# The diagonals of B for TensorE's products: fetched whole from DRAM instead of being built by ScalarE (four-layer visual state-space model, one core)

## The chip, the cores and the metric

The kernel runs on one core of a Trainium2 chip. The metric is the device time of one execution in microseconds, the median of several runs. In the profile PE is TensorE, DVE VectorE, ACT ScalarE, POOL GpSimd, and SP is SyncE, whose queue issues all of this kernel's DMAs.

## The reference

The input is 4 images of 64 x 64 positions with 128 channels. Layers 0, 1 and 3 are selective-scan layers, layer 2 is a gated layer made of matrix products. What matters here is the scan inside a selective-scan layer, cut to its core:

```python
xs = jnp.stack([x0, x1, x0[..., ::-1], x1[..., ::-1]], axis=1)   # 4 directions, 256 channels, 4096 steps
x_dbl = jnp.einsum('bkdl,kcd->bkcl', xs, x_proj_w)
dts, Bs, Cs = jnp.split(x_dbl, [R, R + N], axis=2)               # R = 8, N = 16 states
delta = jax.nn.softplus(jnp.einsum('bkrl,kdr->bkdl', dts, dt_w) + dt_b[None, :, :, None])
def step(h, t):
    x_t, d_t, B_t, C_t = t
    h = jnp.exp(d_t[..., None] * A) * h + (d_t * x_t)[..., None] * B_t[:, :, None, :]
    return (h, jnp.einsum('bkdn,bkn->bkd', h, C_t))
```

For each of the 16 states n and each channel the scan needs, at every step, a decay exp(delta A), an addend delta x B_n, and afterwards a product with C_n summed over the states. B_n and C_n depend on the step and not on the channel. All arithmetic is in float32.

## The kernel before, in words

**Chunks and periods.** The images are taken in two pairs, the three scan layers in turn, which makes 12 turns of one image and one layer. A turn has 4 directions of 8 chunks, and a chunk is 512 steps of 256 channels (two halves m of 128 partitions): 384 chunks. A chunk is worked through in 8 periods, 3,072 in all. Period i takes 4 of the 16 states (quarter q = i // 2) for one of the two halves. Directions 2 and 3 run backward over the same positions ("back" chunks) and use rows that a forward chunk left in DRAM.

**A period.** ACT makes four decays `da` (`decay`, L854). DVE makes four scans `h` (`scan`, L870), two on "side 0" and two on "side 1". For side 0 the addend comes from TensorE: `pair_db` (L845) multiplies the transposed `duT` (delta x) with diagonal matrices of B, so that one product gives delta x B_n for two states at once, in the PSUM tile `dbp`, of which there is one. For side 1 ACT copies delta x into PSUM (`lift`, L862) and DVE multiplies it there with B's rows `bb`, spread over all partitions (L983, L984). POOL multiplies `h` with C's rows `cb` (`times_c`, L882) into `hc`; in periods 0, 2, 4 and 6 it also adds the two sides (L884). PE sums `hc` over the states in `yp` (`add_up`, L895), always that of the period before. ACT saves the last column of `h` as `state` (L878).

**The diagonals.** `diagonals` (L837) builds one block `diag` for a quarter: 4 groups of 128 steps, in each the 128 x 128 identity scaled by B's column of two states, interleaved. ACT does this in 8 scalings of [128 x 128], two of every four in a period; each takes its scale from `bt`, the transpose of B's rows, which PE makes with four transposes (L797) in the prologue and ACT copies out of PSUM (L802). The blocks have two buffers.

**The rest of the work.** While a chunk runs, `prologue` prepares the next one piece by piece (at the half periods listed in `PIECES`): it loads `xs`, projects it to `xd` (8 rows of dt, 16 of B, 16 of C, for two directions) or loads `xd` from DRAM for a back chunk, makes `delta` (softplus with two table loads on ACT), stores `xd` to DRAM (`xd_d`), and makes `du` (POOL) and `duT` (PE, ACT). `spread` (L821) fetches `bb` (512 KB) and `cb` (1 MB) for a quarter from `xd_d`, one row for all partitions; each has two buffers. Between these the steps of the other layers' work run (`between`, called through `other`): norms, products, convolution, and their loads and stores, among them `x_col_d` (L430), stored in pieces of 32 bytes.

**What sets the order.** The program is scheduled by hand: every engine, and SP's queue, executes its instructions in the order in which this code writes them, and waits in place for what it needs. SP therefore waits, in its one queue, for buffers to come free.

Of the kernel before, what the change touches and what calls it, by code (L numbers as in the profile page):

```python
# [13 lines left out]
F32 = mybir.dt.float32  # L14
AF = mybir.ActivationFunctionType
# [14 lines left out]
WP = W + 2  # L30

CQ = 4

PAIRED = (0, 2, 4, 6)

# [29 lines left out]
def vss_stack_kernel(ctx: ExitStack, tc: tile.TileContext, x: bass.AP, weights, out: bass.AP, n_batch=B, layers=(0, 1, 2, 3)):  # L65
# [640 lines left out]
        return [S[a:z] for a, z in zip([0] + marks[1:], marks[1:] + [len(S)])]  # L706


    turns = []
    for e in range(0, n_batch, 2):  # L710
        for i in (0, 1, 3):
# [2 lines left out]
    for turn, (e, i) in enumerate(turns):  # L714

        for nth, k in enumerate((1, 3, 0, 2) if turn else (0, 1, 3, 2)):
            for ci in range(NCH):
                s = SimpleNamespace(turn=turn, e=e, v=wt[i], layer=i, nth=nth, k=k, ci=ci)
                s.c = NCH - 1 - ci if k >= 2 else ci
                s.columns, s.back = k % 2 == 1, k >= 2  # L720
                s.end = 0 if s.back else CH - 1
                s.step = slice(None, None, -1 if s.back else 1)
                s.first, s.last = ci == 0, ci == NCH - 1
                s.flip = len(chunks) % 2
                s.diag, s.cb, s.bb, s.h, s.hc = {}, {}, {}, {}, {}
                chunks.append(s)
    per_turn = K * NCH

# [27 lines left out]
    def scans(pool, ring, deep, psum):  # L756
# [4 lines left out]
        def prologue(s):  # L761


            lane, v = lanes[s.e % 2], s.v
            s.xs = ring.tile([P, 2, CH], F32, tag="xs", name="xs")
            nc.sync.dma_start(out=s.xs, in_=(lane.x_col if s.columns else lane.x_row)[:, :, cols(s.c)])
            if s.first:
                s.dt = pool.tile([R, DI], F32, tag="dt", name="dt_w")
                nc.sync.dma_start(out=s.dt, in_=weights[s.layer][1][:, s.k * DI : (s.k + 1) * DI])
            yield  # L770


            s.xd_d = lane.xd[s.k % 2][s.c]
            s.xd = pool.tile([2 * NX, CH], F32, tag="xd", name="xd")
            if s.back:
                nc.sync.dma_start(out=s.xd[:NX], in_=s.xd_d[1])
                yield
            else:
                ps = psum.tile([P, CH], F32, tag="misc", name="ps_x")
                for m in range(2):  # L780
                    nc.tensor.matmul(ps[: 2 * NX], v["xp"][:, s.k % 2, m, :], s.xs[:, m], start=(m == 0), stop=(m == 1))
                yield
                nc.scalar.copy(s.xd, ps[: 2 * NX])
            s.delta = pool.tile([P, 2, CH], F32, tag="delta", name="delta")
            halves = (s.flip, 1 - s.flip)
            for m in halves:
                ps = psum.tile([P, CH], F32, tag="misc", name="ps_dt")
                nc.tensor.matmul(ps, s.dt[:, m * P : (m + 1) * P], s.xd[:R], start=True, stop=True)  # L788
                yield
                func = AF.Identity if m == halves[0] else AF.Softplus  # L790
                nc.scalar.activation(s.delta[:, m], ps, func, bias=v["dtb"][:, s.k, m : m + 1])  # L791
            m = halves[0]
            nc.scalar.activation(s.delta[:, m], s.delta[:, m], AF.Softplus)  # L793
            nc.scalar.preload_act_table_set("natural_log_exp_and_others")
            ps = psum.tile([P, 4, NX], F32, tag="misc", name="ps_bt")
            for j in range(4):
                nc.tensor.transpose(ps[:, j, :], s.xd[:NX, j * P : (j + 1) * P], ident[:NX, :NX])  # L797
            yield
            if not s.back:
                nc.sync.dma_start(out=s.xd_d.rearrange("k r t -> (k r) t"), in_=s.xd)  # L800
            s.bt = pool.tile([P, 4, N], F32, tag="bt", name="bt")
            nc.scalar.copy(s.bt, ps[:, :, R : R + N])  # L802
            s.du = pool.tile([P, 2, CH], F32, tag="du", name="du")
            for m in halves:
                nc.gpsimd.tensor_mul(s.du[:, m], s.delta[:, m], s.xs[:, m])  # L805
                yield
            s.duT = pool.tile([P, 4, 2, P], F32, tag="duT", name="duT")
            for m in halves:
                ps = psum.tile([P, 4, P], F32, tag="misc", name="ps_duT")
                for j in range(4):  # L810
                    nc.tensor.transpose(ps[:, j, :], s.du[:, m, j * P : (j + 1) * P], ident)  # L811
                yield
                nc.scalar.copy(s.duT[:, :, m, :], ps)  # L813
            yield
# [13 lines left out]
            q = i // 2  # L828
            return q, (i + q + s.flip) % 2

        def diagonals(s, q, half):

            if half == 0:
                s.diag[q] = pool.tile([P, 4, P, 2], F32, tag="diag", name="diag")
            for t in (2 * half, 2 * half + 1):
                for j in range(2):
                    nc.scalar.activation(  # L837
                        s.diag[q][:, t, :, j], ident, AF.Copy, scale=s.bt[:, t, CQ * q + j : CQ * q + j + 1]
                    )

        def pair_db(s, i):
            q, m = place(s, i)
            s.db = psum.tile([P, CH, 2], F32, tag="dbp", name="dbp")
            for t in range(4):
                nc.tensor.matmul(  # L845
                    s.db[:, t * P : (t + 1) * P, :], s.duT[:, t, m, :], s.diag[q][:, t], start=True, stop=True
                )
# [74 lines left out]
        pro = prologue(s)  # L922
        for _ in pro:
            pass
        for q, half in ((0, 0), (0, 1), (1, 0)):
            diagonals(s, q, half)
        spread(s, 0, 0)
        spread(s, 0, 1)
        pair_db(s, 0)
# [5 lines left out]
        for at, (s, i) in enumerate(periods):  # L935
            then = periods[at + 1] if at + 1 < len(periods) else None
            if i == 0:
                nxt = chunks[at // 8 + 1] if at // 8 + 1 < len(chunks) else None
                if nxt:
                    pro, nxt.dt = prologue(nxt), s.dt  # L940
                s.state = pool.tile([P, 2, N], F32, tag="state", name="state") if s.first else before[0].state
                if at % (8 * per_turn) == 0:
                    segments = [(steps, len(steps), frm, to) for steps, frm, to in meanwhile(s.turn)]

            def piece(number):

                if nxt and number in PIECES:
                    next(pro)

            def other(number):  # L950

                gone = at % (8 * per_turn) * 4 + number
                for todo, count, frm, to in segments:
                    while todo and count - len(todo) < count * (gone - frm) / (to - frm):
                        todo.pop(0)()

            da_next = [None, None]
            spreads = (s, i // 2 + 1) if i < 7 else (nxt, 0)
            if i % 2 == 0 or not spreads[0]:
                spreads = None  # L960
            if then:
                da_next[0] = decay(*then, 0)
            if before:
                save(*before, 1)
            if spreads:
                spread(*spreads, 0)
            scan(s, i, 0, 0, da[0], s.db[:, :, 0])
            other(0)
            scan(s, i, 0, 1, da[0], s.db[:, :, 1])
            times_c(s, i, 0)  # L970
            if before:
                add_up(*before, 0)
            if then:
                pair_db(*then)
            piece(2 * i)
            other(1)
            if spreads:
                spread(*spreads, 1)
            if then:
                da_next[1] = decay(*then, 1)  # L980
            save(s, i, 0)
            du, db = dv[i % 2], dv[1 - i % 2]
            nc.vector.tensor_mul(db, du, s.bb[i // 2][:, 0])  # L983
            nc.vector.tensor_mul(du, du, s.bb[i // 2][:, 1])  # L984
            scan(s, i, 1, 0, da[1], db)
            other(2)
            scan(s, i, 1, 1, da[1], du)
            times_c(s, i, 1)
            if then:
                lift(*then)  # L990

            q, half = (i + 2 + i % 2) // 2, 1 - i % 2
            if q < 4:
                diagonals(s, q, half)
            elif nxt:
                diagonals(nxt, q - 4, half)
            if i < 2 and full:
                leave(*full.pop(0))
            if before:
                add_up(*before, 1)  # L1000
            piece(2 * i + 1)
            other(3)
            da = da_next
            before = (s, i)
            if then and then[0].turn != s.turn:
                assert not any(todo for todo, *_ in segments)
# [101 lines left out]
```

## Time and profile before

| | |
|---|---|
| median of 3 runs | 22,745.52 us (22,731.7 to 22,749.28) |
| the profiled execution | 22,741.48 us; its span 22,739.6 us |
| TensorE's granted clock, mean | 0.959 |
| busy | PE 87%, DVE 86%, POOL 85%, ACT 82% |
| DMA | 3,060 MB in 2,437,559 packets, 42.5% of the 16 engines' time |
| ACT, scalings for diag (L837) | 12,288 of 401 ns, 3,952.1 us |
| POOL, hc (L882) | 6,144 of 2,361 ns, 14,411.8 us |
| DVE, scans (L870) | 12,288 of 1,201 to 1,263 ns |
| bb and cb loads (L821) | 1,536 of 512 KB and 1,536 of 1,024 KB |

A row of a group gives its line, engine, operation, output <- inputs, shapes and count, then busy time and the mean of one, then how long the engine stood idle just before and what ended that. A row of the waits gives who waited, for whom, the total in us, how often and the longest. A row of the timeline gives start and duration in us. Releasers are inferred, and a wait for several things is put down to the one that came last by the profile. A row of stretches gives the window, its length, the busy time (and number of instructions) of PE, PEld, DVE, ACT and POOL, the granted clock, the DMA engines' busy share, and GB/s.

### The profile page before, as it was taken

The page shows a single profiled execution, that of the slowest core. Times are in us where ns is not written, and L with a number is a line of the kernel's source. Part 1 is how long each engine was busy: PE and PEld are TensorE (multiplying, and loading weights), DVE is VectorE, ACT ScalarE, POOL GpSimd, SP SyncE. Part 2 cuts the span into 40 slices and gives each one's busy share as a digit, 9 for nine tenths or more (in the row PEclk, how much of TensorE's full clock was granted, in tenths as well). Part 3 has the DMA queues.
Part 4 walks back from the last instruction along what each step waited for, and adds up shares of the span by engine and source line. Part 5 has one row for each costly group of instructions (what it writes and reads, how often), then busy time and mean ns, then how long its engine had stood idle before and what let it go on. Part 6 is the DMA issues. An engine that isn't in the chain of part 4 may idle for free. (4 is left out here: it accounts for less than half of the span.)

```text
span 22739.6 us, 217018 instructions
## 1 busy us (share of the span) xinstructions
PE 19888.1 (87%) x58234; PEld 10543.0 (46%) x58234; DVE 19492.9 (86%) x20186; ACT 18595.2 (82%) x40022; POOL 19252.4 (85%) x8862
## 2 busy tenths in 40 slices
PE   7898898898888888888888888888988888888887
PEld 3444444444444444444444444444444444444443
DVE  5999888888887887888899898898888878878996
ACT  5888888888887887788788788888888878878887
POOL 5999888888887887888889888898888878878996
PEclk8999999999999999999999999999999999999999
DMA  4444444444334434434533544444443443344333
GB/s 106 151 146 149 133 135 146 134 135 144 128 130 129 133 128 124 141 132 139 139 139 138 137 142 138 133 148 133 135 143 126 128 131 134 126 129 143 137 136 106
DMA packets 2437559, 3060.10 MB, mean 135 GB/s; under 512 B 1753840, under 2 KB 1790064, under 8 KB 2238192
## 3 DMA queue, kind: packets, MB, share of 16 engines
q1 hardware_dynamic: 2436336, 3046.22, 42.5%
q8 instruction: 472, 7.73, 0.1%
q14 instruction: 751, 6.15, 0.1%
HBM read 2784.41 MB, written 261.49 MB: 134 GB/s over the span
## 5 line engine op out<-in xcount | busy, mean ns | idle before, releaser
L882 POOL TENSOR_TENSOR hc<-h,cb 128x1024 f32<-128x1024 f32 x6144 | 14411.8, 2361 | 3101.8 <-DVE h L870 1904.4
L895 PE MATMUL yp<-hc,ident 128*128 128x512 f32 x18432 | 9102.8, 621 | 661.2 <-POOL hc L884 447.5
L854 ACT ACTIVATE da<-delta,w 128x512 f32<-128x512 f32 x12288 | 8149.0, 713 | 684.1 <-DVE h L870 671.8
L870 DVE TENSOR_TENSOR_SCAN h<-da,state,dbp 128x512 f32<-128x512 f32 x5376 | 6574.0, 1261 | 1384.8 <-PE dbp L845 1100.3
L845 PE MATMUL dbp<-diag,duT 128*128 128x256 f32 x24576 | 6143.1, 394 | 1314.4 <-DVE h L870 1178.4
L870 DVE TENSOR_TENSOR_SCAN h<-da,state,dv 128x512 f32<-128x512 f32 x5376 | 6585.5, 1263 | 0.0
L845 PEld LDWEIGHTS dbp<-diag,duT 128*128 128x128 f32 x24576 | 4686.5, 195 | 3725.0 <-issue 2165.5
L895 PEld LDWEIGHTS yp<-hc,ident 128*128 128x128 f32 x18432 | 3488.9, 197 | 5003.4 <-issue 3651.1
L837 ACT ACTIVATE diag<-ident,bt 128x128 f32<-128x128 f32 x12288 | 3952.1, 401 | 0.0
L884 POOL TENSOR_TENSOR hc<-hc 128x1024 f32<-128x1024 f32 x1536 | 3621.9, 2358 | 120.4
L983 DVE TENSOR_TENSOR dv<-dv,bb 128x512 f32<-128x512 f32 x3072 | 2087.0, 679 | 837.9 <-ACT dv L862 704.4
L862 ACT COPY dv<-du 128x512 f32<-128x512 f32 x3072 | 1799.9, 586 | 1137.5 <-DVE h L870 1129.4
L984 DVE TENSOR_TENSOR dv<-dv,bb 128x512 f32<-128x512 f32 x3072 | 2116.5, 689 | 0.0
L402 PE MATMUL gap<-halo,cw 128*128 128x512 f32 x3456 | 1657.1, 604 | 17.3 <-ACT wide L385 6.8
L870 DVE TENSOR_TENSOR_SCAN h<-da,dbp 128x512 f32<-128x512 f32 x768 | 893.5, 1201 | 203.1 <-PE dbp L845 166.5
L788 PE MATMUL ps_dt<-xd,dt_w 8*128 8x512 f32 x1536 | 888.7, 659 | 147.6 <-ACT delta L791 78.5
L805 POOL TENSOR_TENSOR du<-delta,xs 128x512 f32<-128x512 f32 x768 | 978.5, 1274 | 32.7 <-ACT delta L793 32.7
L402 PEld LDWEIGHTS gap<-halo,cw 128*128 128x128 f32 x3456 | 641.1, 192 | 743.9 <-issue 697.3
L878 ACT COPY state<-h 128x2 f32<-128x2 f32 x5376 | 964.6, 179 | 0.0
L870 DVE TENSOR_TENSOR_SCAN h<-da,dv 128x512 f32<-128x512 f32 x768 | 894.7, 1203 | 0.0
L413 ACT ACTIVATE wide<-gap,w 128x512 f32<-128x512 f32 x192 | 131.9, 687 | 826.1 <-PE gap L402 826.1
L813 ACT COPY duT<-ps_duT 128x512 f32<-128x512 f32 x768 | 440.9, 574 | 182.6 <-PE ps_duT L811 181.2
(122 smaller groups left out, 11955.2 us busy)
## 6 DMA issues: line engine op xcount, KB each, us to landing
cb<-xd_d SPq DMA_DIRECT2D x1536, 1024.0 KB
bb<-xd_d SPq DMA_DIRECT2D x1536, 512.0 KB
xs<-x_row_d SPq DMA_DIRECT2D x192, 512.0 KB
xs<-x_col_d SPq DMA_DIRECT2D x192, 512.0 KB
x_col_d<-down SPq DMA_DIRECT2D x192, 256.0 KB
x_row_d<-wide SPq DMA_DIRECT2D x96, 512.0 KB
y_d<-y_sb SPq DMA_DIRECT2D x96, 512.0 KB
y<-y_d SPq DMA_DIRECT2D x96, 512.0 KB
```

The costliest lines, as they stand in the source:

```text
L402: nc.tensor.matmul(z.ps, z.cw[:, m, t, :], z.halo[c][:, dy : dy + RPC, dx : dx + W], start=(t == 0), stop=(t == 8),)
L805: nc.gpsimd.tensor_mul(s.du[:, m], s.delta[:, m], s.xs[:, m])
L837: nc.scalar.activation(s.diag[q][:, t, :, j], ident, AF.Copy, scale=s.bt[:, t, CQ * q + j : CQ * q + j + 1])
L845: nc.tensor.matmul(s.db[:, t * P : (t + 1) * P, :], s.duT[:, t, m, :], s.diag[q][:, t], start=True, stop=True)
L854: nc.scalar.activation(da[:, j], s.delta[:, m], AF.Exp, scale=s.v["a"][:, s.k, m, n : n + 1])
L862: nc.scalar.copy(dv[i % 2], s.du[:, place(s, i)[1]])
L870: nc.vector.tensor_tensor_scan(s.h[i, side][:, j, s.step], da[:, j, s.step], db[:, s.step], init, ALU.mult, ALU.add)
L882: nc.gpsimd.tensor_mul(hc, s.h[i, side], s.cb[i // 2][:, 2 * side : 2 * side + 2, :])
L884: nc.gpsimd.tensor_add(hc, hc, s.hc[i, 0])
L895: nc.tensor.matmul(getattr(s, f"yp{m}"), ident, s.hc[i, side][:, j], start=opens and j == 0, stop=i == end and side == 1 and j == 1,)
L983: nc.vector.tensor_mul(db, du, s.bb[i // 2][:, 0])
L984: nc.vector.tensor_mul(du, du, s.bb[i // 2][:, 1])
```

## The change

Two areas in DRAM, one for even and one for odd chunks, are zeroed at the start. Each holds for a quarter 512 rows of 258 floats; element t * 258 + j is the place of B of step t and state j, and the same area read as 4 groups of 128 (of 129) rows of 256 floats has these places on the interleaved diagonals. In the prologue of every chunk two DMAs write the rows of B (states j = 0 and 1 of each quarter) element by element into these places, and `diagonals` becomes one DMA from there, 512 KB in rows of 1 KB. ACT's scalings, PE's transposes of `xd` and ACT's copy of `bt` go. `xd`'s store moves from after the softplus to ahead of it, `xd`'s load for back chunks moves up beside that of `xs`, and the blocks are asked for in the first half of every even period, for two quarters later.

```diff
+DIAG = 2 * P + 2
...
+    diag_d = []
+    zero = y_sb.rearrange("p m l -> p (m l)")[:, : N // CQ * 4 * DIAG]
+    nc.vector.memset(zero, 0.0)
+    for j in range(2):
+        diag_d.append(keep.tile([N // CQ, CH * DIAG], F32, name=f"diag_d{j}"))
+        nc.sync.dma_start(
+            out=diag_d[j].rearrange("q (p c) -> p q c", p=P), in_=zero.rearrange("p (q c) -> p q c", q=N // CQ)
+        )
...
+                s.diag_d = diag_d[s.flip]
...
-            yield
             s.xd_d = lane.xd[s.k % 2][s.c]
             s.xd = pool.tile([2 * NX, CH], F32, tag="xd", name="xd")
             if s.back:
                 nc.sync.dma_start(out=s.xd[:NX], in_=s.xd_d[1])
+            yield
+            if s.back:
                 yield
...
                 nc.tensor.matmul(ps, s.dt[:, m * P : (m + 1) * P], s.xd[:R], start=True, stop=True)
                 yield
+                if m == halves[0]:
+                    if not s.back:
+                        nc.sync.dma_start(out=s.xd_d.rearrange("k r t -> (k r) t"), in_=s.xd)
+                    rows = s.diag_d.rearrange("q (t c) -> q t c", c=DIAG)
+                    for j in range(2):
+                        nc.sync.dma_start(out=rows[:, :, j], in_=s.xd[R + j : R + N : CQ])
...
-            ps = psum.tile([P, 4, NX], F32, tag="misc", name="ps_bt")
-            for j in range(4):
-                nc.tensor.transpose(ps[:, j, :], s.xd[:NX, j * P : (j + 1) * P], ident[:NX, :NX])
             yield
-            if not s.back:
-                nc.sync.dma_start(out=s.xd_d.rearrange("k r t -> (k r) t"), in_=s.xd)
-            s.bt = pool.tile([P, 4, N], F32, tag="bt", name="bt")
-            nc.scalar.copy(s.bt, ps[:, :, R : R + N])
...
-        def diagonals(s, q, half):
-            if half == 0:
-                s.diag[q] = pool.tile([P, 4, P, 2], F32, tag="diag", name="diag")
-            for t in (2 * half, 2 * half + 1):
-                for j in range(2):
-                    nc.scalar.activation(
-                        s.diag[q][:, t, :, j], ident, AF.Copy, scale=s.bt[:, t, CQ * q + j : CQ * q + j + 1]
-                    )
+        def diagonals(s, q):
+            s.diag[q] = pool.tile([P, 4, P, 2], F32, tag="diag", name="diag")
+            nc.sync.dma_start(
+                out=s.diag[q].rearrange("p t c n -> p t (c n)"),
+                in_=s.diag_d[q].rearrange("(t p c) -> p t c", t=4, c=2 * P)[:P],
+            )
...
             if then:
                 pair_db(*then)
+            if i % 2 == 0:
+                if i < 4:
+                    diagonals(s, i // 2 + 2)
+                elif nxt:
+                    diagonals(nxt, i // 2 - 2)
             piece(2 * i)
...
-            q, half = (i + 2 + i % 2) // 2, 1 - i % 2
-            if q < 4:
-                diagonals(s, q, half)
-            elif nxt:
-                diagonals(nxt, q - 4, half)
```

More of the change, by code (lines that the diff above doesn't have):

```diff
@@ L924, in scans @@
             pass
-        for q, half in ((0, 0), (0, 1), (1, 0)):
-            diagonals(s, q, half)
+        for q in range(2):
+            diagonals(s, q)
         spread(s, 0, 0)
@@ L990, in scans @@
                 lift(*then)
-            q, half = (i + 2 + i % 2) // 2, 1 - i % 2
-            if q < 4:
-                diagonals(s, q, half)
-            elif nxt:
-                diagonals(nxt, q - 4, half)
             if i < 2 and full:
```

## The prediction

> **What bounds the kernel now.** I read the engines' totals first, then the waits, then the timeline, and last stretches of a microsecond or two around single transfers.
>
> ```profile
> PE 19888.1 (87%) x58234; PEld 10543.0 (46%) x58234; DVE 19492.9 (86%) x20186; ACT 18595.2 (82%) x40022; POOL 19252.4 (85%) x8862
> ```
>
> No engine bounds it alone. There are 3072 periods (384 chunks of 8), so a period takes 22,739.6 / 3072 = 7.40 us; DVE is busy 6.35 of it, POOL 6.27, ACT 6.05. The timeline of DVE shows how short a period gets when nothing else interferes:
>
> ```profile
> 12029.24 2.45 DVE L870 TENSOR_TENSOR_SCAN h<-da,state,dbp 128x512 f32<-128x512 f32 x2
> ...
> 12035.14 2.43 DVE L870 TENSOR_TENSOR_SCAN h<-da,state,dbp 128x512 f32<-128x512 f32 x2
> ```
>
> Here it is 12035.14 - 12029.24 = 5.9 us, DVE without a gap. The other 1.5 us of the mean come where side work (the next chunk's prologue, the layer steps) makes some engine late. The waits say which:
>
> ```profile
> POOL hc L882 <- DVE h L870: 1904.4, 1302, 9.8
> DVE h L870 <- PE dbp L845: 1266.8, 658, 9.6
> DVE dv L983 <- ACT dv L862: 704.4, 346, 6.4
> POOL hc L882 <- DMA cb<-xd_d: 368.1, 78, 10.9
> DVE cen L245 <- ACT gap L242: 290.2, 139, 10.7
> ```
>
> DVE's rows on ACT (704.4, 290.2, and 114.5, 77.2, 32.9, 25.8 and some 25 in smaller ones) make 1,270 us. Waiting for DMA is small today, 368 us on cb, because SP's queue runs early:
>
> ```profile
> SPq L821 <- DVE dv L984: 6728.0, 1106, 17.2
> SPq L821 <- POOL hc L882: 6662.9, 1249, 11.6
> ```
>
> SP spends 13.4 ms waiting for a free bb or cb buffer, and issues each load the moment the buffer is free, about two periods ahead of its use. That lead is what the change spends.
>
> **What goes.** 12,288 scalings and 384 copies of bt leave ACT:
>
> ```profile
> L837 ACT ACTIVATE diag<-ident,bt 128x128 f32<-128x128 f32 x12288 | 3952.1, 401 | 0.0
> L802 ACT COPY bt<-ps_bt 128x64 f32<-128x64 f32 x384 | 73.3, 191 | 29.8 <-PE ps_bt L797 28.8
> ```
>
> That is 4,025 us, 1.3 us of ACT a period (82% to 64%). What it is worth is only what ACT's lateness costs now: 1,270 us on DVE plus 125.6 us that PE's dbp products waited for diag, 1,396 in all. It is not worth all of this, since in quick stretches the next engine is just as full (12060 to 12120 us: DVE busy 58.6 us of 60, POOL 58.4, ACT 56.2). Ends: 0 and 1,396; I take the middle, **-700**. PE loses the 1,536 records of transposes of xd (172 us busy, weight loads beside others); half of it on the path, **-86** (ends 0 and 172).
>
> **What comes, and its cover.** SP gets per chunk four fetches of a diagonal block (512 KB, pieces of 1 KB) and two writes of B's rows (2,048 single floats each).
>
> The fetches. In SP's order one stands, every second period, ahead of the next bb and cb. It waits for PE's products from the block that it overwrites, the dbp of period i+1, done about 5.2 us into period i (in the stretch above dbp began 2.6 us after the first scan and took 2.0; I add 0.6 for busy stretches). Behind it wait bb and cb, and POOL waits for cb. Rates: around one cb load the stretches show
>
> ```profile
> 12032.50:12033.00 0.50, 0.50 (x5) 0.42 (x4) 0.50 (x2) 0.50 (x2) 0.50 (x1) 1.00 1.12 459
> 12033.00:12033.50 0.50, 0.50 (x4) 0.37 (x2) 0.50 (x1) 0.14 (x2) 0.50 (x1) 1.00 0.98 410
> ```
>
> (last column GB/s), so about 400: diag 1.5 us (nothing here shows pieces of 1 KB; 1.3 at the full rate, 2 at 256 GB/s), bb 1.3, cb 2.6, with 0.6 ahead of the first byte and 1 for landing: 7.0 us. cb lands 5.2 + 7.0 = 12.2 us after the even period's start; POOL wants it two periods and two scans later, 14.8 + 2.45 = 17.2. No wait in the mean, and none at 5.9 us a period (4.6 + 7.0 = 11.6 against 14.2). The cover is 2.6 to 5 us where it was 8 to 10. The blocks themselves are used 20 us later and cost nothing.
>
> A store in front of cb eats that cover. x_col_d is stored in 8,192 pieces of 32 B, and the timeline of SP and the stretches show what that does:
>
> ```profile
> 4395.65 1.30 SPq L430 DMA_DIRECT2D x_col_d<-down  x1
> 4397.05 7.40 SPq L821 DMA_DIRECT2D cb<-xd_d  x1
> ```
> ```profile
> 4402.00:4404.00 2.00, 2.00 (x4) 0.72 (x3) 2.00 (x2) 0.55 (x2) 2.00 (x2) 0.71 1.87 46
> ```
>
> The store runs at 46 GB/s: 32 B / 46 = 0.70 ns a piece, or 11.1 ns on each of 16 engines, 5.7 us in all, and the next issue takes 7.40 us instead of 0.32. In today's trace POOL then stood idle for 4.7 us, until 4410.14 (the view names a scan as the releaser, but the scans that this hc needed had ended at 4404.1). There are 192 such stores; with the thinner cover I give each 0.5 us (ends 0 and 3.1): **+96**.
>
> The writes are the main cost. Each is 2,048 pieces of 4 B. I price a piece as a 32 B one, 11.1 ns on its engine (nothing nearer is in the trace; the ends are half and twice that). How many engines share it no view shows. The source is four rows of xd, so I take four engines: 512 x 11.1 = 5.7 us a write, 11.4 for both; over sixteen it would be 2.9, on one 45. The Trainium skill, page "DMA: Bandwidth & Descriptors", section "Why a DMA increments its semaphore by 16 and not by 1", says that a DMA issued from SP is split over the largest number of engines up to 16 that divides the slowest dimension of both sides, which makes four here, too; no row of this trace shows it. The same page's "Rules for kernel authors" speaks against the whole idea: a strided last dimension becomes one descriptor per element, and one should rearrange; it names no price.
>
> The writes stand in SP's order in period 3, between bb and cb of quarter 2, behind the fetch that SP issues 5.2 us into period 2. So this cb lands 0.6 + 1.5 + 1.3 + 0.4 (xd's store, 160 KB) + 11.4 + 2.6 + 1 = 18.8 us after it, 24.0 after the start of period 2, where POOL wants it at 17.2: POOL stalls 6.8 us once a chunk, at period 4. PE's queue carries that on: the yp products of hc of period 5 stand ahead of the dbp for period 7. At 7.4 us a period POOL does hc twice, the sum, du and hc (2.36 x 4 + 1.27 = 10.7) from 9.2 after period 4's start, ending 5.1 into period 6; yp 0.9 and dbp 1.9 end 0.5 late for DVE. At 5.9 us a period cb lands 4.6 + 18.8 = 23.4 after period 2's start, the same steps end 10.5 into period 6, yp and dbp at 13.3, and DVE waits 7.4. How the chunks divide between the two no view says; I weigh slow to quick 3 to 2, which is a judgement: 0.6 x 0.5 + 0.4 x 7.4 = 3.2 us a chunk (ends 0 and the 6.8 of POOL): 384 x 3.2 = **+1,230**.
>
> Small things: the fetch for the next chunk's quarter 0 also waits for both writes (landed 22 us after period 2's start, 2 us after its other wait); bb and cb of quarter 3 queue behind it, and cb still lands 2.6 us early. xd's load for the backward chunks and its store move about a period earlier: nothing. Zeroing DRAM at the start moves 2 x 2.1 MB at 400 GB/s ahead of the first weights: **+10** (ends 0 and 20).
>
> **Sum** against the profiled execution's 22,741.5 us (4 us under the median of 22,745.5, so it stands for it): 22,741.5 - 700 - 86 + 96 + 1,230 + 10 = 23,291, **23,290 us**, 2.4% slower.
>
> **Rivals.** *Absorbed* (faster): the writes are spread over 16 engines, or POOL makes good the stall out of the 1,904 us in which it waits for scans today. Then what is left is ACT's relief. With no stall at all it is 22,741.5 - 786 + 106 = 22,060; with the 0.5 us of the slow case in every chunk, 22,250; with a partial stall up to 22,650. It decides at (786 - 106) / 384 = 1.8 us a chunk on the path. For it: POOL is idle 9.1 us a chunk. Against it: POOL and DVE are full in just those stretches in which ACT is not late.
>
> *Dear pieces* (much slower): a 4 B write costs twice a 32 B one. The pair takes 22.8 us, the stall is 18 us, and no idle time holds that: it adds the 11.4 of the dearer pair to every chunk, 23,290 + 384 x 11.4 = 27,670.
>
> *No relief*: ACT is nobody's bound, the 786 are 0, the stall as in the forecast: 24,080.
>
> *Nothing*: both sides cancel to within 0.2%, which is about what a measurement of this kernel can tell from no change.
>
> **How the numbers follow.** Forecast 0.40 (22,800 to 24,000), no relief 0.10, dear pieces 0.07, absorbed 0.38, nothing 0.05. So faster by over 0.2% 0.38, within 0.05, slower 0.57. The range reaches down into the absorbed case, to 22,150, and up to 24,500, near the full 6.8 us stall on the path (22,741.5 - 786 + 106 + 2,611 = 24,670); outside are the best of the absorbed case and the dear pieces, 2 in 10. The likeliest case's own range is 22,800 to 24,000.
>
> **What would show it.** Right: ACT near 64%; POOL's wait for DMA cb grows from 368 us to 2,000 or more, in one period of eight; the issue behind the second write takes 5 us or more; POOL's wait for scans shrinks; DVE's waits for ACT halve, while those for PE dbp grow. Wrong: POOL's wait for cb stays under 800 us (the writes are cheap or spread), or DVE's wait for PE dbp falls.

## The result, and the profile after

The changed kernel takes 25,330.18 us (median of four runs, 25,323.29 to 25,331.35) against 22,746.18 (four runs by then): a ratio of 1.114 [1.112, 1.115], 11% slower. The forecast was 2.4% slower, with a range that ended at 24,500. The profiled execution took 25,323.29 us (span 25,321.5), so it stands for the median.

The engines' totals after, in the same columns as before:

```profile
PE 20176.9 (80%) x56698; PEld 10684.4 (42%) x56698; DVE 19524.6 (77%) x20187; ACT 15202.8 (60%) x27350; POOL 19195.7 (76%) x8862
```

ACT lost 3,392 us of work, and DVE and POOL do what they did. PE is 289 us busier, although its transposes of `xd` are gone; the last section comes back to this. Every engine waits more. The rows of the waits that answer to those of before:

```profile
POOL hc L894 <- DMA cb<-xd_d: 3719.5, 500, 22.4
...
DVE h L882 <- PE dbp L857: 2838.8, 753, 24.5
...
POOL hc L894 <- DVE h L882: 1554.2, 879, 17.1
...
DVE h L882 <- POOL hc L894: 825.3, 278, 12.7
...
DVE dv L1001 <- ACT dv L874: 530.7, 267, 5.8
```

POOL's wait for `cb` grew from 368 to 3,720 us, in about one period of a chunk (500 times in 384 chunks). DVE's wait for `dbp` grew from 1,267 to 2,839 and its wait for POOL from 93 to 825, while its largest wait for ACT fell only from 704 to 531. The row of before on POOL:

```profile
DVE h L870 <- POOL hc L882: 92.8, 42, 8.9
```

SP's queue hardly waits for `bb` and `cb` buffers any more (765 us for POOL in place of 6,663), but for the products that free a diagonal block, and for the writes:

```profile
SPq L848 <- PE dbp L857: 13111.3, 1156, 20.5
...
SPq L848 <- DMA diag_d<-xd: 1062.1, 364, 8.7
```

One chunk in the timeline of SP, where the second column is the time that an issue takes:

```profile
12004.19 0.37 SPq L848 DMA_DIRECT2D diag<-diag_d  x1
12004.66 0.46 SPq L836 DMA_DIRECT2D bb<-xd_d  x1
12005.16 0.42 SPq L808 DMA_DIRECT2D xd_d<-xd  x1
12005.64 7.58 SPq L811 DMA_DIRECT2D diag_d<-xd  x2
12013.32 5.87 SPq L836 DMA_DIRECT2D cb<-xd_d  x1
```

The second write's issue is held until 12013.2, and that of `cb` behind it for another 5.87 us. The stretches of one microsecond, with the DMA engines' share and GB/s in the last two columns, show what the DMA engines did meanwhile:

```profile
12010.00:12011.00 1.00, 0.00 (x0) 0.00 (x0) 1.00 (x1) 1.00 (x1) 0.00 (x0) 1.00 0.43 2
...
12013.00:12014.00 1.00, 0.00 (x0) 0.00 (x0) 1.00 (x2) 1.00 (x2) 0.66 (x1) 0.50 0.38 1
...
12019.00:12020.00 1.00, 1.00 (x3) 0.45 (x2) 0.62 (x1) 0.99 (x2) 0.00 (x0) 0.78 0.39 1
...
12022.00:12023.00 1.00, 1.00 (x6) 0.90 (x5) 0.00 (x0) 0.99 (x3) 0.00 (x0) 1.00 1.02 418
```

From 12010 to 12020 the core moves 1 or 2 GB/s, about 10 us of nothing but single floats; then `cb` comes at 418 GB/s. POOL's timeline closes the chain:

```profile
12011.30 2.36 POOL L894 TENSOR_TENSOR hc<-h,cb 128x1024 f32<-128x1024 f32 x1 [2.05 <-DVE h L882]
12024.21 4.68 POOL L894 TENSOR_TENSOR hc<-h,cb 128x1024 f32<-128x1024 f32 x2 [10.55 <-DMA cb<-xd_d]
```

POOL stands idle for 10.55 us, until `cb` has landed. The mean length of the eight periods of a chunk, which I took from the starts of each period's first scan over the whole trace, says where it ends: before 8.04, 7.27, 6.97, 7.29, 7.61, 7.52, 7.40, 6.48 us; after 7.96, 7.24, 7.01, 7.32, 7.56, **9.26, 12.45**, 6.46. All of the loss is in periods 5 and 6, one and two behind the `cb` that came late.

### The profile page after: what moved, and what is told of

It reads as the page before. It is cut to its first block, busy times and chain, and to the rows that moved or that the text cites. A ratio compares the mean times of both kernels' runs of the same rounds, so it can differ in the third digit from the quotient of the medians.

```text
span 25321.5 us, 205410 instructions
## 1 busy us (share of the span) xinstructions
PE 20176.9 (80%) x56698; PEld 10684.4 (42%) x56698; DVE 19524.6 (77%) x20187; ACT 15202.8 (60%) x27350; POOL 19195.7 (76%) x8862
## 5 line engine op out<-in xcount | busy, mean ns | idle before, releaser
L907 PE MATMUL yp<-hc,ident 128*128 128x512 f32 x18432 | 9525.1, 645 | 2970.9 <-POOL hc L896 2831.9
L907 PEld LDWEIGHTS yp<-hc,ident 128*128 128x128 f32 x18432 | 3608.8, 205 | 7511.0 <-issue 3672.2
L826 PEld LDWEIGHTS ps_duT<-ident,du 128*128 128x128 f32 x3072 | 478.6, 170 | 455.0 <-issue 395.8
```

Of the source, the lines that this page charges most:

```text
L907: nc.tensor.matmul(getattr(s, f"yp{m}"), ident, s.hc[i, side][:, j], start=opens and j == 0, stop=i == end and side == 1 and j == 1,)
```

## The experiments

The edits are against the changed kernel unless said otherwise; ratios are to the kernel before.

**1. The relief by itself.** The kernel before, without ACT's scalings: `dbp` multiplies with two constant blocks of zeros, so B's diagonals are left out of the result; `bt` is still made.

```diff
...
-                for j in range(2):
-                    nc.scalar.activation(s.diag[q][:, t, :, j], ident, AF.Copy, scale=s.bt[...])
...
+                s.diag[q] = fixed[q % 2]
```

> The kernel before, with ACT's 12,288 scalings left out: the products read two constant blocks, and no block is built, written or fetched. This is the relief of ACT by itself. Theory A (the prediction's term): ACT's lateness costs part of the 1,396 us of waits, so the time falls by about 700, to 22,050 (22,746 less 350 to 1,050). Theory B (ACT was nobody's bound: after the change the periods 0 to 4 and 7 of a chunk are as long as before): within 150 us of 22,746.

Measured: 22,393.6 us, 0.985 [0.984, 0.987]. Taking away 3,950 us of ACT's work is worth 344 us, just under the lower end of the first theory. DVE's waits for ACT, all rows together, fell from 1,286 to 1,013 us, so most of them do not come from the scalings.

**2. Without the two writes.** The fetches stay and read the zeros that the area was filled with, so the diagonals are left out of the result.

```diff
-                    for j in range(2):
-                        nc.sync.dma_start(out=rows[:, :, j], in_=s.xd[R + j : R + N : CQ])
```

> The changed kernel without the two writes of B's rows; the fetches stay and read zeros. Theory A (the writes alone are the loss, because cb of quarter 2 stands behind them in SP's queue): POOL's wait for cb falls from 3,720 us to under 900, and the time to that of the scalings left out, plus at most 200 us. Rival (the fetches and SP's wait for PE ahead of bb and cb are a good part of the loss): the time stays over 23,500 and POOL's wait for cb over 1,500 us.

Measured: 22,552.3 us, 0.992 [0.990, 0.993], as the first theory said.

```profile
DVE h L879 <- PE dbp L854: 1187.2, 635, 14.6
...
POOL hc L891 <- DMA cb<-xd_d: 638.4, 244, 10.7
...
DVE h L879 <- POOL hc L891: 66.0, 37, 5.4
```

So the two writes cost 25,330 - 22,552 = 2,778 us, 7.2 a chunk, and the fetches, less the transposes that are gone, 22,552 - 22,394 = +159. Together with the relief, -344 + 159 + 2,778 = +2,593; the change measured +2,584. (The three add up by construction; the 9 us are the kernel before, which was measured twice.)

**3. The writes behind cb of quarter 2**, in period 3.

```diff
+            if i == 3 and nxt:
+                write_b(nxt)
```

> The changed kernel with the two writes issued after cb of quarter 2 instead of ahead of it; everything else as it is. Theory A (place in the queue): cb of quarter 2 arrives in time, the fetch for the next chunk's quarter 0 waits for the writes some 8 us longer, cb of quarter 3 is then tight; POOL's wait for cb falls under 1,500 us, time about 23,000. Rival (the writes slow all transfers on the engines that they share, wherever they stand): the time stays over 24,500.

Measured: 23,620.4 us, 1.039 [1.037, 1.041]. Of the writes' 2,778 us 1,710 went, the rest moved:

```profile
DVE dv L1006 <- DMA bb<-xd_d: 1393.3, 355, 17.1
...
POOL hc L896 <- DMA cb<-xd_d: 1151.0, 352, 17.6
```

Next on SP's queue stands the fetch of the next chunk's first block, which must wait for the writes to land, and `bb` and `cb` of quarter 3 stand behind it. Now it is `bb` for which most of the waiting is, 1,393 us in place of 323 in the changed kernel. POOL's wait for `cb` came as the first theory said, the time 600 us above it.

**4. One write for each row**, eight instead of two, to bring more DMA engines to the same pieces.

```diff
+                    for q in range(N // CQ):
+                        for j in range(2):
+                            n = R + CQ * q + j
+                            nc.sync.dma_start(out=rows[q : q + 1, :, j], in_=s.xd[n : n + 1])
```

> The changed kernel with eight writes of one row each instead of two of four rows, in the same place; the same 4,096 pieces. Theory A (a write runs on as many engines as its source has rows, so four): with one row the 512 steps are what is divided, sixteen engines take part, the writes take 3 to 5 us instead of 13.6 and POOL's wait for cb falls under 1,500 us, time about 22,900. Rival (the pieces cost what they cost in the generation of the descriptors, whatever the engines): writes as long as before or longer, time 25,300 or more.

Measured: 25,534.9 us, 1.123 [1.122, 1.125]: no gain, as the rival said. In the timeline of SP the issue alone takes as long as the writes did:

```profile
12049.41 10.51 SPq L813 DMA_DIRECT2D diag_d<-xd  x8
12060.02 1.28 SPq L838 DMA_DIRECT2D cb<-xd_d  x1
```

Eight issues take 10.5 us, 1.3 for 512 pieces, so that `cb` goes out about when it does in the changed kernel.

**5. One write only**, half the pieces; the other state's diagonals are left out of the result.

```diff
-                    for j in range(2):
+                    for j in range(1):
```

> The changed kernel with one of the two writes left out (the blocks lack every second diagonal); half of the pieces, in the same place. Theory A (the price is the time that cb of quarter 2 stands behind pieces, some 2.9 us for 1,000 of them, beyond a slack of a few us): cb lands 5.9 us earlier, POOL's wait for cb falls from 3,720 to about 1,500 us, and of the 7.2 us a chunk that the writes cost, 5 go: time 23,300 (22,900 to 23,700). Rival (a fixed price of having any such write, for instance SP's wait for its landing): time over 24,500.

Measured: 23,258.6 us, 1.023 [1.021, 1.024], as the first theory said. Half of the pieces cost 706 us, a quarter of the 2,778: the cost is not in proportion to the pieces. POOL's wait for `cb`, over the 638 us of experiment 2, tells how:

```profile
POOL hc L894 <- DMA cb<-xd_d: 1785.6, 492, 18.2
```

It grew by 1,148 us, 3.0 a chunk, of which 1.8 reached the time.

**6. The fetch behind cb**, in odd periods, without writes (the diagonals left out of the result, as in 2).

```diff
-            if i % 2 == 0:
+            if i % 2 == 1:
...             (and the block moved below the spread of cb)
```

> No writes, as in the second experiment, and the fetch of a block half a period later in SP's order, behind bb and cb of the odd period instead of ahead of them. Theory A (what the fetches cost, 159 us between the second and the first experiment, is that SP waits for PE ahead of bb and cb): SP runs early again, the cost goes, time 22,400 (up to 22,470). Rival (it is the 0.8 GB more in the DMA engines): time stays at 22,550.

Measured: 22,353.6 us, 0.983 [0.982, 0.984], as the first theory said. The fetches' 159 us are gone; the time is 40 under experiment 1, which still has the transposes.

```profile
POOL hc L891 <- DMA cb<-xd_d: 408.3, 92, 11.0
```

POOL's wait for `cb` is back from 638 to 408 us. So the price of the fetches was their place in the queue, ahead of `bb` and `cb`.

**7. Both behind cb**: the fetch as in 6, the two writes in period 5 behind `cb` of quarter 3.

```diff
+            if i == 5 and nxt:
+                write_b(nxt)
```

> The whole change, with the fetches behind cb as in the sixth experiment and the two writes in period 5 behind cb of quarter 3. Nothing that POOL or DVE needs within two periods stands behind the writes. Theory A (place in the queue is all of it): time within 100 us of the sixth experiment, 22,500, faster than the kernel before. Rival (writes of 13 us a chunk disturb other loads wherever they stand): 23,000 or more.

Measured: 23,236.8 us, 1.022 [1.020, 1.023]. The cure of 6 does not carry over to this place: `cb` is on time (511 us), but the next thing on the queue is late instead:

```profile
PE dbp L859 <- DMA diag<-diag_d: 1032.4, 223, 16.7
```

The fetch of the next chunk's first block waits for the writes, and PE for the fetch; period 7 takes 8.79 us in the mean instead of 6.42 (experiment 6). The time is the rival's, but not its reason: what is late stands behind the writes in the queue.

**8. Written from bt.** Place as in 7, but the source is `bt` (the transposes and ACT's copy are back), so that one transfer of 2,048 pieces of 8 bytes starts from 128 partitions.

```diff
+            places = s.diag_d.rearrange("q (t p c) -> p (q t) c", t=4, p=P)
+            nc.sync.dma_start(out=places[:, :, :2], in_=s.bt.rearrange("p q t c -> p (q t) c")[:, :, :2])
```

> As the seventh, but the writes come from bt as in the kernel before (PE transposes, ACT copies, 245 us of their time back): one DMA of 2,048 pieces of 8 bytes from 128 partitions instead of 4,096 pieces of 4 bytes from 4. Theory A (128 source rows are spread over 16 engines like the 32-byte pieces of x_col_d, at 0.7 ns a piece): the write takes 1.5 to 2 us. Rival (a price by the piece, 2.9 ns, whatever the rows): 6 us. The time is 22,500 to 22,650 by both, since it stands behind cb.

Measured: 22,491.5 us, 0.989 [0.987, 0.991], faster than both kernels. The issue takes 0.37 us, and the stretches around it show the write at about 2 us, part of it under another load:

```profile
12024.12 0.37 SPq L850 DMA_DIRECT2D diag_d<-bt  x1
```
```profile
12024.00:12025.00 1.00, 1.00 (x4) 0.51 (x3) 1.00 (x3) 1.00 (x3) 0.92 (x2) 1.00 0.60 238
12025.00:12026.00 1.00, 1.00 (x6) 0.68 (x5) 1.00 (x2) 1.00 (x4) 1.00 (x1) 1.00 0.90 140
12026.00:12027.00 1.00, 1.00 (x6) 0.71 (x4) 1.00 (x2) 0.98 (x4) 1.00 (x2) 1.00 0.50 7
```

In the third the core is down to 7 GB/s; in the fourth microsecond nothing is left. Four things differ from 7: 128 partitions instead of four rows, 8 bytes instead of 4, half as many pieces, and one transfer instead of two. No run separates them.

**9. Written from DRAM**, at the original place, the 512 steps as the outermost dimension instead of the four rows.

```diff
+                    places = s.diag_d.rearrange("q (t c) -> t q c", c=DIAG)
+                    source = s.xd_d[s.k // 2].rearrange("r t -> t r")
+                        nc.sync.dma_start(out=places[:, :, j], in_=source[:, R + j : R + N : CQ])
```

> The changed kernel with the two writes in their place, but read from xd's rows in DRAM with the step as the outer and the quarter as the inner dimension, so that 512 steps are divided among engines and not four rows; the same 4,096 pieces of 4 bytes in two DMAs. They now wait for the landing of xd's store. Theory A (four engines were the price): at 0.7 to 1 ns a piece both take 3 to 4 us, POOL's wait for cb falls under 1,500 us, time 22,700 to 23,100. Rival (2.5 to 2.9 ns for every single-float piece, however it is divided, as the row by row writes took): 11 us or more as before, time 25,300 or more.

Measured: 25,098.1 us, 1.103 [1.102, 1.105], nearly nothing gained; neither theory is wholly right.

```profile
12005.00:12006.00 1.00, 1.00 (x3) 0.24 (x3) 0.88 (x1) 0.00 (x0) 0.77 (x1) 1.00 0.65 5
...
12007.00:12008.00 1.00, 1.00 (x4) 0.49 (x3) 1.00 (x2) 0.00 (x0) 0.00 (x0) 1.00 0.01 0
```

The pieces do go faster while they go: 5 GB/s is 1,250 pieces a microsecond, against 250 to 500 at 1 to 2 GB/s. But between the bursts the DMA engines stand still (share 0.01), and the writes now also wait for `xd`'s own store (SP, 875.9 us in all). What the transfer does in these gaps the trace does not show.

**10. Slow writes in period 3, fetch behind cb**: 3 and 6 together.

> The whole change with the fetches behind cb (as in the sixth experiment) and the two slow writes of 4-byte pieces in period 3, behind cb of quarter 2. In the seventh they stood two periods later and the next chunk's first block came too late (PE waited 1,032 us for it). Theory A (a place exists where nobody waits for what stands behind the writes: SP runs early, so they go out about 4 us into period 2, are done about 3 us into period 4, and bb and cb of quarter 3 leave then): 22,400 to 22,600, faster than the kernel before. Rival (the writes cost something wherever they stand, since 13 us of a blocked queue never fit): 23,000 or more, with bb or cb of quarter 3 late.

Measured: 22,882.2 us, 1.006 [1.005, 1.008], between the two theories and still slower than before.

```profile
PE dbp L859 <- DMA diag<-diag_d: 776.7, 166, 17.3
```

It is the block of quarter 3 that stands behind the writes here, and period 5, which makes its first products, takes 8.56 us. Wherever the two slow writes stand, something waits behind them: `cb` (changed kernel), `bb` (3), or a block (7, 10).

**11. PE's order**: `dbp` of the next step ahead of the first `yp` of the step before.

```diff
+            if then:
+                pair_db(*then)
             if before:
                 add_up(*before, 0)
-            if then:
-                pair_db(*then)
```

> The kernel after, with one change: in TensorE's order the products of B's diagonals with du (dbp) of the next step stand ahead of the first half of the sums (yp) of the step before; nothing is left out. Two theories of how POOL's wait for the late cb reaches VectorE. Theory A: through PE's in-order queue: the yp products wait for POOL's late hc and the next dbp stands behind them. Then VectorE's scan no longer waits there, its waits for PE's dbp (2,839 us in the kernel after) fall to half, and the time falls to about 24,200 us (some 3 of the 7.2 us a chunk). Theory B: it is POOL itself and the h buffers that the scans need back, so the order on PE does not matter: 25,200 to 25,400 us, and dbp's waits turn into waits for POOL's hc.

Measured: 24,978.2 us, 1.098 [1.096, 1.100], between the two theories. DVE's wait for `dbp` fell by 1,002 us, two thirds of what the first named, but the time fell by 352 only:

```profile
DVE h L882 <- PE dbp L857: 1836.7, 709, 24.2
...
DVE dv L1001 <- ACT dv L874: 862.1, 381, 7.2
```

The waits for ACT's `dv` grew by 331, those for `da` from 56 to 334. By periods, 5 and 6 together fell from 21.7 to 20.0 us, and the other six grew by 0.8, so that 0.9 us a chunk reached the time. The exchange takes only one `hc` of POOL (2.36 us) out of the way: the next `dbp` still stands behind the second half of the `yp` of one step further back, and these need a late `hc` too. So this run does not say how much of the stall goes through PE's queue; DVE's waits by period, below, say more.

**12. bt early**: as 8, with the transposes right after x's, the write in period 3 and two periods between it and the fetch that needs it.

> Nothing is left out. The diagonals are written from bt (128 partitions, 2,048 pieces of 8 bytes, one transfer), the fetch of the next diag stands behind cb, and the two transposes of B are made right after x's transposes, so that the write can stand in period 3, behind cb of quarter 2, and the fetch of the next chunk's first quarter in period 5, two periods behind the write. Theory A: what held the version with the late write (22,491 us) above the version without writes (22,354 us) is the wait of PE for the last diag of a chunk (185 us); with two periods between write and fetch it falls under 40 us and the time is 22,380 to 22,440 us. Theory B: the difference is the two transposes, their eviction by ScalarE and the write's traffic, wherever they stand: 22,470 to 22,560 us. Bound for both: before's 22,746 us is not reached.

Measured: 22,486.2 us, 0.989 [0.987, 0.991], the same as 8 and what the second theory said. PE's wait for a block fell only from 185 to 139 us; what holds both about 135 us above experiment 6 goes with the transposes, the copy and the write as such, wherever they stand. How it divides among them was not measured.

## Why the prediction was wrong

**The mechanism was right as far as POOL, and incomplete from there to DVE.** `cb` is late at quarter 2, once a chunk, behind two writes that move nothing but single floats, and POOL stalls. From POOL to DVE the prediction named one path, PE's queue, in which the `yp` products of period 5 stand ahead of the `dbp` for period 7. That path is there: over experiment 2, DVE's wait for `dbp` grew by 1,652 us (2,839 - 1,187), 4.3 a chunk, in the trace all of it between the first scans of periods 6 and 7. A second path was not in the prediction: a scan needs its `h` buffer back from POOL (there are four, so period 6 writes over those of period 4). DVE's wait for POOL's `hc` grew by 759 us (825 - 66), 2.0 a chunk, nearly all of it between the first scans of periods 5 and 6. Most signs came: the issue behind the second write took 5.87 us (5 or more), POOL's wait for `cb` passed 2,000, its wait for scans shrank (1,904 to 1,554), and DVE's wait for `dbp` grew. Two missed: DVE's wait for ACT did not halve (1,286 to 1,152), and ACT fell to 60% of a longer span, where 64% was named.

**The writes' own price held.** 11.4 us was predicted for both. Over 373 chunks of the trace (without the first and last few), the last packet of `cb` of quarter 2 ends in the mean 26.7 us after the first scan of period 2 with the writes and 15.7 without (experiment 2): 11.0. That four engines share it, the packets of the trace support (experiment 2, then the changed kernel):

```profile
DMA packets 3249537, 3868.92 MB, mean 172 GB/s; under 512 B 1778448, under 2 KB 2601104, under 8 KB 3050256
DMA packets 4825481, 3875.29 MB, mean 153 GB/s; under 512 B 3354384, under 2 KB 4177040, under 8 KB 4626192
```

The writes add 1,575,936 packets under 512 bytes, 4,104 a chunk: 4,096 floats, and 4 more for each write. The same count gives 16 more for each write of experiments 4, 8 and 9. Read as one word for each engine that takes part, which no view says, the changed kernel's writes ran on four engines and the others on sixteen; 11.0 us are then 10.7 ns a piece and engine, for the 11.1 that were taken. But the 2.9 us that the prediction gave to sixteen engines did not come: in experiments 4 and 9 `cb` still landed 11.6 and 10.3 us later than without writes, with an issue of 10.5 us in the one and pauses in the other. The Trainium skill, page "DMA: Bandwidth & Descriptors", section "Why a DMA increments its semaphore by 16 and not by 1", lets the slowest dimension of both sides choose the number of engines; experiment 9 changed that dimension from 4 to 512, and its bursts were faster by about three, which agrees, while its total did not fall. The same page's "Rules for kernel authors" names one descriptor for each element where the last dimension is strided, which agrees with the 4,096 packets a chunk.

**The landing was 2.7 us late.** 24.0 us after period 2's start was predicted, 26.7 measured. The fetch was put at 5.2 us into the period, from a quick stretch plus 0.6; in the mean over the trace it goes out at 6.1. The steps behind it take 20.6 us and not 18.8. Without the writes they take 9.5, where the prediction has 7.0 and 0.4 for `xd`'s store, so the loads and what stands between them were priced too short: `cb` was given 0.6 + 2.6 + 1 = 4.2 us from its issue. No run shows the 0.6 and the 1 by themselves; to the last packet it took 4.6 us in the median in the kernel before, and 7.0 behind a fetch and `bb` (experiment 2). The cover that was put at 5 us was therefore about 2: POOL comes to this `cb` at 17.6 where it is early (experiment 6), and it lands at 15.7. "No wait in the mean" hid the chunks in which there is one; experiment 2 less experiment 6 prices the place of the fetch at 199 us.

**The step that failed most is the one from POOL's stall to the time.** A stall of 6.8 us was predicted and 3.2 of it charged, +1,230, so that 3.6 were to be absorbed; measured are a stall of 8.0 (3,720 - 638 us, over 384) and a cost of 7.2, +2,778, so 0.8 was absorbed. Of the 4.0 us a chunk that are missing, 1.2 (470 us in all) are the longer stall and 2.8 (1,080 us) the absorption. It came from the case at 7.4 us a period, which made DVE 0.5 us late at period 7 and nowhere else and so let 6.3 of 6.8 us go, with a weight of 0.6 that was a judgement. In its place the runs show, over experiment 2, 5.1 us lost ahead of period 7 and 2.2 ahead of period 6. Two reasons can be read: `cb` lands 12.6 us into period 4 and not 9.2, and the prediction's own chain (10.7 + 0.9 + 1.9 us, against the 22.0 from period 4 to period 7 in experiment 2) then ends about 4 us late, by this estimate; and the `h` buffers were not in it. The runs with different stalls give the share directly:

| | POOL's added wait for cb, us a chunk | added time, us a chunk |
|---|---|---|
| one write (5) | 3.0 | 1.8 |
| other order on PE (11) | 6.8 | 6.3 |
| from DRAM (9) | 7.7 | 6.6 |
| changed kernel | 8.0 | 7.2 |
| row by row (4) | 8.7 | 7.8 |

(All over experiment 2, whose order on PE is not that of 11.) About 1 us is absorbed, whatever the size. POOL's idle time says the same from its side. Without the writes POOL idles 22,536 - 19,224 = 3,312 us, 638 for `cb`: 2,673 for everything else. After, it is 25,322 - 19,196 = 6,126, 3,720 for `cb`: 2,406. Of 3,081 us of stall POOL made good 267. So the "9.1 us a chunk" of idle time on which the rival *absorbed* leaned was hardly a reserve. My reading is that POOL spends it waiting for work that itself comes later when POOL is late; no run tests this by itself.

**The relief was half its term.** -700 was taken as the middle between 0 and 1,396; the scalings measured -344. DVE's rows on ACT are the sum that was taken as recoverable (1,270 us in the prediction, 1,286 with the smallest rows); four fifths of them (1,013) stayed with 1.3 us less of ACT's work in every period. Of the terms beside it, the transposes (-86) were not measured by themselves: experiment 6, without them and with the fetches behind `cb`, is 40 us under experiment 1. The stores' +96 cannot be told from the rest of the 199 that the fetch's place costs, and the zeroing was not measured.

**The range** ended below the result because its top let one thing go wrong at a time: the full 6.8 us on the path with the full relief, or no relief with 3.2 us. Both ends were in the text, and together, 22,741.5 + 106 + 2,611 = 25,460, they would have held 25,330.

## What to carry to other kernels

Price a DMA by its pieces and by what stands behind it in its queue: the same floats, written from 128 partitions in pieces of 8 bytes, with the write and the fetches behind the loads that have a date, turned 11% slower into 1% faster. Where every engine is nearly full, as here, do not count an engine's idle time as slack: of stalls of 3 to 9 us about 1 us was made good. Follow a late transfer along every way to the next engine, the buffers that must come back as well as the queue. And take the start of a queued step and the length of a load from the mean of a trace and not from its quickest stretch, for a cover of a few microseconds is decided by one or two.

## What the runs showed of the hardware

A write of single floats holds SP's own issue, not only the DMA engines: the second write and the `cb` behind it took 7.58 (both writes) and 5.87 us to issue where a load takes 0.32 to 0.46; in the mean of all chunks the second write alone took 6.8 and this `cb` 5.9. More transfers did not help (1.3 us for a row of 512 pieces, eight in 10.5 us), nor did a piece rate of 1,250 in a microsecond, since bursts came with pauses.

TensorE's granted clock fell with the stall. Over the run it is 0.915 against 0.959 before and 0.965 without the writes. Averaged over the chunks of the trace by period, it is 0.75 in period 6 and 0.90 in period 5, where experiment 2 has 0.97 in both; in the other six periods the two runs agree within 0.01. With the same 56,698 instructions PE is busy 640 us longer than in experiment 2 (20,176.9 against 19,536.9), 1.7 us a chunk. How much of the 7.2 us a chunk this makes, no run separates. In the stretches above the clock is 0.50 from about 12013 to 12019, but PE's idle time ahead of that was ended by ACT's `delta` and not by `cb`:

```profile
12014.20 2.07 PE L804 MATMUL ps_dt<-xd,dt_w 8*128 8x512 f32 x2 [4.49 <-ACT delta L813]
12016.20 5.29 PE L907 MATMUL yp<-hc,ident 128*128 128x512 f32 x8
...
12023.06 1.88 PE L907 MATMUL yp<-hc,ident 128*128 128x512 f32 x4
```

Four `yp` products take 1.88 us here at a clock of 1.00, so eight would take some 3.8; these eight take 5.29.
